# Attention exponentials shared between ScalarE and VectorE: a shorter polynomial with a phase in the row maxima, and another spacing of VectorE's sets

## The chip, the cores and the metric

The kernel runs on one core of a Trainium2 chip. The metric is the device time of one execution in microseconds (us); each version is run several times and the median is taken. Beside it there is one execution recorded by the hardware profiler, whose span and instructions are quoted here. TensorE (PE) multiplies matrices into PSUM, ScalarE (ACT) evaluates functions such as exp, VectorE (DVE) does elementwise arithmetic and reductions, GpSimd (POOL) copies and issues some DMAs, SyncE (SP) issues most DMAs.

## The reference

Four graph layers over 3327 nodes with 128 features and a 3327 x 3327 matrix adj. Nearly all the time is in the first, an attention of 128 heads with 8 features each, in which adj is added to the logits twice:

```python
def _L0_gnn_ref(x, spatial_encoding, edge_encoding, Wq, Wk, Wv, Wo):
    q = (x @ Wq.T).reshape(d, n, h)
    k = (x @ Wk.T).reshape(d, n, h)
    v = (x @ Wv.T).reshape(d, n, h)
    a = jnp.einsum('dnh,dmh->dnm', q, k) * scale
    a = a + spatial_encoding + edge_encoding
    a = jax.nn.softmax(a, axis=2)
    out = jnp.einsum('dnm,dmh->dnh', a, v)
    out = out.reshape(n, h * d)
    return out @ Wo.T
...
x = _layernorm(x + _L0_gnn_ref(x, adj, adj, Wq, Wk, Wv, Wo))
x = _layernorm(x + _L1_gnn_ref(x, adj, W, b))
x = _layernorm(x + _L2_gnn_ref(x, adj, W_in, W_out))
x = _layernorm(x + _L3_gnn_ref(x, adj, W, b))
```

So 128 x 3327 x 3327 exponentials are taken, about 1.4 thousand million.

## The kernel before

A first stage (to about 320 us) projects queries, keys and values and writes them to scratch memory in DRAM. It also stores, for 512 rows at a time, the row maxima of adj split in two parts (`store_tops`, L220 to L228); these go into the queries' image as extra rows, so that the matmul of the scores subtracts them. The last stage (from about 10000 us) runs the other layers. Between them `attention` (L412) holds the change.

**Tiling.** The queries are cut into seven columns of 476 (`CW`), the keys into four runs of 7, 7, 6 and 6 tiles of 128 (`KBS`). A *block* is one column with one run, 28 blocks in all; the kind of a block (`kb`, 0 to 3) is its run. Each block goes through all 128 heads, four heads making a *group* (`GROUP`), 32 groups a block.

**Sets.** For one head the key tiles of a block are taken in three *sets* (`SETS`, L446): 3, 2 and 2 tiles in blocks of seven, 2, 2 and 2 in blocks of six. Each set has its own PSUM buffer (`sc0`, `sc1`, `sc2`), only one of each. `exponents` (L609) issues, for one set, the score matmuls (L625) and then an exponential from PSUM to an SBUF tile `e`: on ScalarE (L633, with scale 2), or, for some third sets, on VectorE (`vector_exp`, L583). The scores stay in PSUM from head to head: each head's matmul adds its own product and takes the last head's away. So the matmul of the next head into a buffer must wait until the exponential has read it.

**VectorE's exponential.** L589 scales the scores to an integer (from PSUM), L590 and L592 separate exponent and mantissa, and one product for each constant of `POLY` follows (L595), five before. L589 is issued at once; the others are put in the list `vec`, and `vector_work` (L600) takes them out one by one, against a planner's clock: `clock[0]` advances a fixed amount a set (0.95 or 0.84 us), `clock[1]` by the estimated cost of VectorE's work. Tiles `ey` and `et` have one buffer each.

**Who takes a set.** `on_vector(kb, g)` (L448) gives VectorE the third set of a group's first head, in all groups of the second kind, in three of four of the first kind and in seven of eight of the last two.

**Weighing.** One group later `weigh` (L640) multiplies the exponentials of four heads with the values into the one PSUM buffer `o` (L651). Where in the group's twelve sets the weighings stand is given by tables: `FULL` for the first kind, `PLACES` for the others, `FIRST` for a block's first group (L455 to L458). Before a weighing that needs the third set, `weigh` takes the rest of that group's products out of `vec`. Every three groups `flush` (L658) adds `o` to an accumulator on VectorE (L662, L664), and the next weighing waits for that.

**Other work on VectorE in this stage.** In the groups ahead of a block of the first kind `copy_queries` (L506) makes three copies of the next group's queries (L510 to L512). `background_work` (L544) sums and transposes pieces of adj for the later layers: at the last head of every eighth group two operations (L202, L207), and four groups later three more (L209, L216, L217), for 91 pieces.

PE, ACT, POOL and DVE run in the order of this Python loop (`manual_schedule`): an instruction stands behind all that were issued before it on its engine.

Of the kernel before, what the change touches and what calls it, by code (L numbers as in the profile page):

```python
# [10 lines left out]
F32 = mybir.dt.float32  # L11
F32R = mybir.dt.float32r
I32 = mybir.dt.int32
AF = mybir.ActivationFunctionType
ALU = mybir.AluOpType
# [5 lines left out]
GROUP = 4  # L21
# [4 lines left out]
CW = 476  # L26
# [1 line left out]

POLY = (-0.12145248055458069, 1.287218689918518, 0.8447736501693726, 0.7106341123580933, 0.24892811477184296)
UPPER, LOWER = 0x7F800000, 0x7FFFFF
EXPONENT, QUARTER = 0x40000000, 0x3E800000
EPS = 1e-5
# [16 lines left out]
def kernel(ctx: ExitStack, tc: tile.TileContext, x, adj, wq, wk, wv, wo,  # L51
# [14 lines left out]
    nc = tc.nc  # L66
# [13 lines left out]
    KBS = [(0, 7), (7, 7), (14, 6), (20, 6)]  # L80
    assert KBS[-1][0] + KBS[-1][1] == T

    def tokens(t):
        return P - 1 if t == T - 1 else P
# [9 lines left out]
    def flat_ap(dram, at, pattern):  # L94

        f = dram.rearrange("r c -> (r c)")
        if isinstance(at, int):
            base = f[at:at + 1]
        else:
            base = f[ds(at, 1)]  # L100
        return bass.AP(base.tensor, base.offset, pattern)
# [118 lines left out]
    def store_tops(pool, u, top, n):  # L220

        hi = pool.tile([P, 4], F32R, name="rhi")
        nc.vector.tensor_copy(hi, top)
        lo = pool.tile([P, 4], F32R, name="rlo")
        nc.vector.tensor_tensor(lo, top, hi.bitcast(F32), ALU.subtract)
        for row, sb in enumerate((hi, lo)):
            for i in range(P // n):
                nc.gpsimd.dma_start(out=flat_ap(lead_s[u], row * SUPER + i * P, [[1, n], [n, 4]]),  # L228
                                    in_=sb[n * i:n * i + n, :].bitcast(F32))
# [18 lines left out]
    with tc.tile_pool(name="pw", bufs=1) as pw, tc.tile_pool(name="pa", bufs=2) as pa, \  # L248
# [110 lines left out]
        d = 0  # L359
# [30 lines left out]
        top = pw.tile([P, 2], F32, name="top")  # L390
# [21 lines left out]
    def attention():  # L412
        with tc.tile_pool(name="acc", bufs=1) as accp, tc.tile_pool(name="kq", bufs=3) as kq, \
# [14 lines left out]
            blocks = [(min(c, N - CW), kb) for c in range(0, N, CW) for kb in range(len(KBS))]  # L428
# [16 lines left out]

            SETS = {7: [(0, 3), (3, 2), (5, 2)], 6: [(0, 2), (2, 2), (4, 2)]}  # L446

            def on_vector(kb, g):  # L448

                return g % 4 != 0 if kb == 0 else KBS[kb][1] == 7 or g % 8 != 0  # L450

            FULL = ((0, 2, 4, 4, 7, 7, 9), (0, 0, 3, 7, 7, 10, 10), (0, 0, 3, 6, 6, 9, 9), (0, 0, 3, 6, 7, 10, 10))  # L455
            PLACES = {7: (1, 1, 4, 6, 8, 10, 10), 6: (0, 2, 4, 6, 8, 10)}

            FIRST = {7: (4, 4, 5, 7, 7, 10, 10), 6: (4, 4, 7, 7, 10, 10)}  # L458

# [54 lines left out]
            def tile_at(nt, i):  # L514

                return (i % 2, i // 2, (i // 2) + ((nt + 1) // 2 if i % 2 else 0))

            def load_values(b, g):
                k0, nt = KBS[blocks[b][1]]
                if g % 2 == 0:  # L520
                    pairs[b, g // 2] = kq.tile([P, 2, 7 * 32], F32, name="vs", bufs=2)
                    nc.sync.dma_start(out=pairs[b, g // 2].rearrange("p a c -> p (a c)")[:, 0:2 * nt * 32],
                                      in_=flat_ap(v_img, k0 * HD + g * nt * 32, [[T * HD, P], [1, 2 * nt * 32]]))
                vs = pairs[b, g // 2].rearrange("p a c -> p (a c)")[:, g % 2 * nt * 32:(g % 2 + 1) * nt * 32]
                vp = v_pads[(b * NHG + g) % 3]
                nc.gpsimd.tensor_copy(  # L526
                    vp[:, 32:32 + nt * GROUP * 32].rearrange("p (x c) -> p x c", c=32)[:, :, 0:H],
                    vs.rearrange("p (x c) -> p x c", c=H))
                return vp
# [27 lines left out]
            def prepare(b, d):  # L557

                n = b * NHG + d // GROUP
                if d % GROUP == 0:  # L560
                    while any(of is None for _, of, _ in vec):
                        vec.pop(0)[2]()
                    if n + 2 < len(groups):
                        heads[groups[n + 2]] = load_heads(*groups[n + 2])
                    if blocks[b][1] == 0:
                        nc.sync.dma_start(out=qimg[d // GROUP],
                                          in_=heads[groups[n]][1].bitcast(F32)[0:64].rearrange("p a c -> p (a c)"))
                    if n + 1 < len(groups):
                        values[groups[n + 1]] = load_values(*groups[n + 1])
                    while stores:  # L570
                        store(*stores.pop(0))
                    background(n)


                if n + 1 < len(groups) and blocks[groups[n + 1][0]][1] == 0 \
                        and d % GROUP == 1 - on_vector(blocks[b][1], d // GROUP):
                    vec.extend(copy_queries(*groups[n + 1]))
                if d % GROUP == 3:
                    background_work(n)

            vec = []

            def vector_exp(e, x, of):  # L583


                y = ex.tile([P, 2, CW], F32, name="ey")
                t = ex.tile([P, 2, CW], F32, name="et")
                yi, ti = y.bitcast(I32), t.bitcast(I32)
                nc.vector.tensor_scalar(yi, x, -58 * math.log(2.0), 2 ** 24 / math.log(2.0), ALU.max, ALU.mult)  # L589
                vec.append((0.7, of, lambda: nc.vector.tensor_scalar(ti, yi, UPPER, EXPONENT, ALU.bitwise_and,  # L590
                                                                 ALU.bitwise_xor)))
                vec.append((0.7, of, lambda: nc.vector.tensor_scalar(yi, yi, LOWER, QUARTER, ALU.bitwise_and,  # L592
                                                                 ALU.bitwise_or)))
                for i, a in enumerate(POLY):
                    vec.append((1.2, of, lambda i=i, a=a: nc.vector.scalar_tensor_tensor(  # L595
                        e, e if i else y, a, t if i == len(POLY) - 1 else y, ALU.add, ALU.mult)))

            clock = [0.0, 0.0]

            def vector_work(b):  # L600

                while vec and clock[1] < clock[0]:
                    cost, _, step = vec.pop(0)
                    step()
                    clock[1] += cost
                clock[0] += 0.95 if KBS[blocks[b][1]][1] == 7 else 0.84
                clock[1] = max(clock[1], clock[0] - 1)

            def exponents(b, d, si):  # L609
                kb = blocks[b][1]  # L610
                nt = KBS[kb][1]
                t0, n = SETS[nt][si]
                s = sc[si]
                if d == 0:
                    for i in range(n):
                        tl = tile_at(nt, t0 + i)[2]
                        for j, (q0, w) in enumerate(subs):
                            nc.tensor.matmul(s[:, i, q0:q0 + w], lhsT=edges[b][0:w, j, tl * P:(tl + 1) * P],
                                             rhs=ident[0:w, 0:w], is_transpose=True,
                                             start=(j == 0), stop=True, skip_group_check=True)  # L620
                kt, qt = heads[b, d // GROUP]
                k = d % GROUP
                for i in range(n):
                    rg, pos, _ = tile_at(nt, t0 + i)
                    nc.tensor.matmul(s[:, i, 0:CW], lhsT=kt[64 * rg:64 * rg + 64, k, pos * P:(pos + 1) * P],  # L625
                                     rhs=qt[64 * rg:64 * rg + 64, k, :],
                                     start=False, stop=True, skip_group_check=True)
                e = ex.tile([P, (3, 2, 2)[si], CW], F32, tag=f"e{si}", name=f"e{si}", bufs=(6, 7, 8)[si])
                if on_vector(kb, d // GROUP) and (d % GROUP, si) == (0, 2):
                    vector_exp(e[:, 0:n, :], s[:, 0:n, 0:CW], (b, d // GROUP))  # L630
                    clock[1] += 1.2
                else:
                    nc.scalar.activation(e[:, 0:n, :], s[:, 0:n, 0:CW], AF.Exp, scale=2.0)  # L633
                for i in range(n):
                    es[b, d, t0 + i] = e[:, i, :]
                if d % (2 * GROUP) == 0 and d // (2 * GROUP) < len(subs) and si == len(SETS[nt]) - 1 \
                        and b + 1 < len(blocks):
                    load_edges(b + 1, d // (2 * GROUP))
# [39 lines left out]
            with tc.manual_schedule(engines={mybir.EngineType.PE, mybir.EngineType.Activation,  # L678
# [8 lines left out]
                for b, d in steps:  # L687
                    prepare(b, d)
                    for si in range(len(SETS[KBS[blocks[b][1]][1]])):
                        vector_work(b)  # L690
                        exponents(b, d, si)
                        if queue:
                            at = (FIRST[len(queue_of)] if d < GROUP else PLACES[len(queue_of)] if blocks[b][1] else
                                  FULL[d // GROUP % 4])
# [462 lines left out]
    with tc.manual_schedule(engines={mybir.EngineType.PE, mybir.EngineType.SP}):  # L1157
# [18 lines left out]
        for t in range(T):  # L1176
            n = tokens(t)
# [15 lines left out]
        for t in range(T):  # L1193
            n = tokens(t)
# [15 lines left out]
        for t in range(T):  # L1210
            n = tokens(t)
# [16 lines left out]
        for t in range(T):  # L1228
            n = tokens(t)
# [35 lines left out]
```

## Time and profile before

| | |
|---|---|
| median of 3 runs | 10760.09 us (10756.05 to 10763.08) |
| span of the profiled execution | 10769.0 us |
| attention stage, first score tile to last weighing | 322 to 10001 us |
| ScalarE's exponentials (L633) | 9968 |
| VectorE's sets (L589) | 784 |
| mean granted TensorE clock | 0.994 |

A busy time is the time in which an engine has an instruction running. The profile gives after each group's busy time the engine's idle time just before it and what ended most of it. The windows view shows one block of each kind (the columns are the window, its length, busy time and instructions of each engine, the granted clock, the DMA share and GB/s):

```profile
1718.00:2085.00 367.00, 359.91 (x2705) 128.50 (x2703) 299.40 (x319) 362.95 (x361) 58.64 (x104) 1.00 0.67 174
2085.00:2453.00 368.00, 367.17 (x2720) 130.72 (x2716) 287.09 (x288) 356.24 (x353) 50.41 (x96) 1.00 0.86 193
2453.00:2775.00 322.00, 319.36 (x2342) 105.44 (x2338) 254.59 (x260) 308.70 (x357) 58.09 (x106) 1.00 0.90 203
2775.00:3095.00 320.00, 318.83 (x2334) 105.54 (x2333) 256.41 (x258) 309.24 (x358) 76.62 (x132) 1.00 0.89 208
```

The engines stand in the order PE, PE weight loads, DVE, ACT, POOL. Blocks of seven tiles take about 368 us, blocks of six about 320 us.

### The profile page before, as it was taken

Reading aid. Unit: us, or ns where it says so; the run is one execution under the profiler, and the core shown is the slowest. Engines: PE = TensorE matmul, PEld = TensorE weight load, DVE = VectorE, ACT = ScalarE, POOL = GpSimd, SP = SyncE. Lnnn points to the kernel's source line nnn. Section 1 sums busy time; section 2 is a strip of 40 time slices with the busy share of each in tenths; the row PEclk is TensorE's granted clock in tenths of the full one; section 3 lists DMA queues with packets and bytes.
Section 4 is the critical chain, followed back from the end, with each engine's and each line's share of the span. In section 5 each row is a group of like instructions: output and inputs, shape, how many; then the busy total and the mean of one; then the engine's idle time right before and its main releaser. Section 6 shows DMA issues by size and latency. Waiting matters only on the chain. (4 is left out here: it accounts for less than half of the span.)

```text
span 10769.0 us, 200811 instructions
## 1 busy us (share of the span) xinstructions
PE 10578.8 (98%) x76941; PEld 4110.9 (38%) x76941; DVE 7959.0 (74%) x8554; ACT 9583.6 (89%) x10447; POOL 1555.0 (14%) x2742
## 2 busy tenths in 40 slices
PE   8899999999999999999999999999999999999999
PEld 5333333333333333333333333333333333333779
DVE  6677788877788778887788777878777777777412
ACT  3799999999999999999999999999999999999400
POOL 0111122111221111211122111121111100001200
PEclk9999999999999999999999999999999999999999
DMA  7678897788976889768888688886888867888676
GB/s 250 187 183 189 205 212 183 178 194 199 211 191 168 199 203 209 192 170 193 198 209 200 156 192 189 198 195 171 194 194 201 195 162 178 181 188 197 220 281 246
DMA packets 1013555, 2116.45 MB, mean 197 GB/s; under 512 B 206760, under 2 KB 730730, under 8 KB 998772
## 3 DMA queue, kind: packets, MB, share of 16 engines
q1 hardware_dynamic: 915358, 1972.12, 75.8%
q0 software_dynamic: 79616, 116.88, 3.7%
q8 instruction: 623, 10.21, 0.4%
q10 hardware_dynamic: 17620, 14.49, 0.4%
q14 instruction: 338, 2.76, 0.1%
HBM read 1863.03 MB, written 239.54 MB: 195 GB/s over the span
## 5 line engine op out<-in xcount | busy, mean ns | idle before, releaser
L633 ACT ACTIVATE e<-sc 128x952 f32<-128x952 f32 (+1 forms) x9968 | 9361.2, 1085 | 322.8 <-PE sc L625 295.0
L651 PE MATMUL o<-e,v_pad 128*32 128x476 f32 (+1 forms) x46592 | 5650.9, 573 | 43.2 <-DVE acc L664 18.6
L625 PE MATMUL sc<-qt,kt 64*128 64x476 f32 x23296 | 4494.8, 440 | 55.8 <-ACT e L633 33.9
L625 PEld LDWEIGHTS sc<-qt,kt 64*128 64x128 f32 x23296 | 2184.3, 184 | 4439.7 <-ACT e L633 3736.3
L595 DVE SCALAR_TENSOR_TENSOR e<-e,ey 128x952 f32<-128x952 f32 x2352 | 2706.5, 1151 | 77.4
L589 DVE TENSOR_SCALAR ey<-sc 128x952 int32<-128x952 f32 x784 | 901.2, 1149 | 1426.5 <-PE sc L625 1389.1
L651 PEld LDWEIGHTS o<-e,v_pad 128*32 128x32 f32 (+1 forms) x46592 | 1035.8, 108 | 1914.8 <-issue 1893.1
L526 POOL COPY v_pad<-vs 128x192 f32<-128x192 f32 (+1 forms) x896 | 439.0, 516 | 8029.8 <-DMA vs<-v_img 6501.4
L595 DVE SCALAR_TENSOR_TENSOR e<-ey 128x952 f32<-128x952 f32 x784 | 903.0, 1152 | 27.2
L595 DVE SCALAR_TENSOR_TENSOR e<-e,et 128x952 f32<-128x952 f32 x784 | 901.5, 1150 | 22.2
L237 POOL DMA_DIRECT2D adjT_s<-at x1352 | 760.4, 570 | 141.5 <-DMA adjT_s<-at 99.2
L590 DVE TENSOR_SCALAR et<-ey 128x952 int32<-128x952 int32 x784 | 519.5, 663 | 26.9
L592 DVE TENSOR_SCALAR ey<-ey 128x952 int32<-128x952 int32 x784 | 518.9, 662 | 27.1
L1101 PE MATMUL bank<-y,eT 128*128 128x128 f32 (+1 forms) x4056 | 473.9, 276 | 0.4 <-DVE h L1223 0.4
L1101 PEld LDWEIGHTS bank<-y,eT 128*128 128x128 f32 (+1 forms) x4056 | 465.3, 192 | 5.7 <-DVE h L1223 0.6
L664 DVE TENSOR_TENSOR acc<-o,acc 128x476 f32<-128x476 f32 x231 | 150.3, 651 | 284.5 <-PE o L651 284.0
L510 DVE TENSOR_SCALAR qt<-qt 32x1428 fp32r<-32x1428 f32 x224 | 201.8, 901 | 93.3 <-DMA qt<-q_s 64.2
L1061 ACT ACTIVATE rstd<-mv,eps 128x1 f32<-128x1 f32 x104 | 30.4, 293 | 265.2 <-DVE mv L1059 265.2
L512 DVE CAST qt<-qt 64x1904 fp32r<-64x1904 f32 x224 | 259.9, 1160 | 7.6
L671 POOL DMA_DIRECT2D o_s<-acc x308 | 200.4, 655 | 35.3 <-DVE acc L664 21.2
L1204 PE MATMUL bank<-a,y 128*128 128x512 f32 (+2 forms) x364 | 145.5, 562 | 0.0
L348 ACT ACTIVATE hi<-pp 128x1024 fp32r<-128x1024 f32 x52 | 52.7, 1024 | 95.4 <-PE pp L292 78.2
(151 smaller groups left out, 2286.6 us busy)
## 6 DMA issues: line engine op xcount, KB each, us to landing
qt<-qimg SPq DMA_DIRECT2D x1344, 476.0 KB
kt<-k_s SPq DMA_DIRECT2D x5320, 96.0 KB
kt<-k_s SPq DMA_DIRECT2D x1764, 128.0 KB
eT<-adjT_s SPq DMA_DIRECT2D x78, 1664.0 KB
qimg<-qt SPq DMA_DIRECT2D x224, 476.0 KB
vs<-v_img SPq DMA_DIRECT2D x224, 224.0 KB
adjT_s<-at POOLq DMA_DIRECT2D x1352, 32.0 KB, 5.0
vs<-v_img SPq DMA_DIRECT2D x224, 192.0 KB
```

The lines of the kernel that those rows point to most:

```text
L237: nc.gpsimd.dma_start(out=flat_ap(adjT_s, (t * P + 32 * q) * NP + c * PIECE, [[NP, 32], [P, ns], [1, P]]), in_=at[32 * i:32 * i + 32].rear ...
L510: return [(0.9, None, lambda: nc.vector.tensor_scalar(qt[32:64, 1:], qf[0:32, 0:GROUP - 1], -1.0, None, ALU.mult)), (0.4, None, lambda: nc ...
L512: (1.2, None, lambda: nc.vector.tensor_copy(qt[64:128], qf[0:64]))]
L526: nc.gpsimd.tensor_copy(vp[:, 32:32 + nt * GROUP * 32].rearrange("p (x c) -> p x c", c=32)[:, :, 0:H], vs.rearrange("p (x c) -> p x c", c=H))
L589: nc.vector.tensor_scalar(yi, x, -58 * math.log(2.0), 2 ** 24 / math.log(2.0), ALU.max, ALU.mult)
L590: vec.append((0.7, of, lambda: nc.vector.tensor_scalar(ti, yi, UPPER, EXPONENT, ALU.bitwise_and, ALU.bitwise_xor)))
L592: vec.append((0.7, of, lambda: nc.vector.tensor_scalar(yi, yi, LOWER, QUARTER, ALU.bitwise_and, ALU.bitwise_or)))
L595: vec.append((1.2, of, lambda i=i, a=a: nc.vector.scalar_tensor_tensor(e, e if i else y, a, t if i == len(POLY) - 1 else y, ALU.add, ALU.m ...
L625: nc.tensor.matmul(s[:, i, 0:CW], lhsT=kt[64 * rg:64 * rg + 64, k, pos * P:(pos + 1) * P], rhs=qt[64 * rg:64 * rg + 64, k, :], start=False ...
L633: nc.scalar.activation(e[:, 0:n, :], s[:, 0:n, 0:CW], AF.Exp, scale=2.0)
L651: nc.tensor.matmul(o[32 * j:32 * j + 32, 0:CW], lhsT=values[b, g][:m, c:c + 32], rhs=es[b, g * GROUP + j, r][:m, :], start=(r == 0 and u = ...
L1101: nc.tensor.matmul(ps[:n, 0:D], lhsT=e[:m, s, :n], rhs=y[:m, s, col:col + D], start=(s == 0), stop=(s == T - 1))
```

## The change

VectorE's polynomial has four constants and products instead of five. A constant `PHASE` is taken off the stored row maxima, so that every score is higher by it; ScalarE's exponential takes twice that off again with its bias. `on_vector` now counts heads: VectorE takes the third set of every fourth head in the first kind of block, of every third head in the second, and of heads 0 and 4 of every seven in the last two. `vector_exp` first takes the products of an earlier set out of `vec`. The places of the weighings in blocks of six move by one set, the query copies enter at a group's first head in all groups, and the planner's clock advances by 0.935 and 0.81.

```diff
-POLY = (-0.12145248055458069, 1.287218689918518, 0.8447736501693726, 0.7106341123580933, 0.24892811477184296)
+POLY = (-0.039287679561190725, 0.7694055213858888, 0.3602062482980112, 0.1471829588776368)
+PHASE = 0.7927868171488225 * math.log(2.0) / 2
...
-        nc.vector.tensor_copy(hi, top)
+        nc.vector.tensor_scalar(hi, top, -PHASE, None, ALU.add)
...
-        nc.vector.tensor_tensor(lo, top, hi.bitcast(F32), ALU.subtract)
+        nc.vector.scalar_tensor_tensor(lo, top, -PHASE, hi.bitcast(F32), ALU.add, ALU.subtract)
...
-            def on_vector(kb, g):
-
-                return g % 4 != 0 if kb == 0 else KBS[kb][1] == 7 or g % 8 != 0
+            def on_vector(kb, d):
+
+                return d % 4 == 0 if kb == 0 else d % 3 == 0 if KBS[kb][1] == 7 else d % 7 in (0, 4)
...
-            PLACES = {7: (1, 1, 4, 6, 8, 10, 10), 6: (0, 2, 4, 6, 8, 10)}
+            PLACES = {7: (1, 1, 4, 6, 8, 10, 10), 6: (1, 3, 5, 7, 9, 11)}
...
                 if n + 1 < len(groups) and blocks[groups[n + 1][0]][1] == 0 \
-                        and d % GROUP == 1 - on_vector(blocks[b][1], d // GROUP):
+                        and d % GROUP == 0:
                     vec.extend(copy_queries(*groups[n + 1]))
...
             def vector_exp(e, x, of):
+                while any(to is not None for _, to, _ in vec):
+                    vec.pop(0)[2]()
...
-                clock[0] += 0.95 if KBS[blocks[b][1]][1] == 7 else 0.84
+                clock[0] += 0.935 if KBS[blocks[b][1]][1] == 7 else 0.81
...
-                if on_vector(kb, d // GROUP) and (d % GROUP, si) == (0, 2):
+                if si == 2 and on_vector(kb, d):
                     vector_exp(e[:, 0:n, :], s[:, 0:n, 0:CW], (b, d // GROUP))
                     clock[1] += 1.2
                 else:
-                    nc.scalar.activation(e[:, 0:n, :], s[:, 0:n, 0:CW], AF.Exp, scale=2.0)
+                    nc.scalar.activation(e[:, 0:n, :], s[:, 0:n, 0:CW], AF.Exp, bias=-2 * PHASE, scale=2.0)
```

## The prediction

> **What bounds the kernel now.** I read the busy shares first, then the groups by shape, then VectorE's and ScalarE's timelines inside the attention stage (320 to 10000 us, where the change lies), and last the waits of PE.
>
> ```profile
> PE 10578.8 (98%) x76941; PEld 4110.9 (38%) x76941; DVE 7959.0 (74%) x8554; ACT 9583.6 (89%) x10447; POOL 1555.0 (14%) x2742
> ```
>
> ```profile
> L633 ACT ACTIVATE e<-sc 128x952 f32<-128x952 f32 x8176 | 7324.3, 1015 | 202.3 <-PE sc L625 197.8
> L633 ACT ACTIVATE e<-sc 128x1428 f32<-128x1428 f32 x1792 | 2512.6, 1402 | 120.5 <-PE sc L625 97.2 <-DMA qt<-q_s 23.2
> L589 DVE TENSOR_SCALAR ey<-sc 128x952 int32<-128x952 f32 x784 | 901.2, 1149 | 1426.5 <-PE sc L625 1389.1
> L590 DVE TENSOR_SCALAR et<-ey 128x952 int32<-128x952 int32 x784 | 519.5, 663 | 26.9
> L592 DVE TENSOR_SCALAR ey<-ey 128x952 int32<-128x952 int32 x784 | 518.9, 662 | 27.1
> L595 DVE SCALAR_TENSOR_TENSOR e<-e,ey 128x952 f32<-128x952 f32 x2352 | 2706.5, 1151 | 77.4
> ```
>
> The first fence is the page's busy time, the second the groups by shape (busy us, mean ns of one, idle time before and its releaser). PE's 98% has modelled ends, so it does not say that PE is the limit. ScalarE is idle only 323 us before its exponentials. VectorE waits 1389 us for fresh scores before L589, 1.8 us for each of 784 sets: that is its slack. In time, in a block of six key tiles:
>
> ```profile
> 2577.34 1.15 DVE L589 TENSOR_SCALAR ey<-sc 128x952 int32<-128x952 f32 x1 [1.38 <-PE sc L625]
> 2583.35 1.24 DVE L202 STREAM_TRANSPOSE at<-ai 128x1024 f32<-128x1024 f32 x1
> 2584.51 1.18 DVE L207 TENSOR_REDUCE pmax<-ai 128x4 f32<-128x1020 f32 x1
> 2585.61 0.64 DVE L664 TENSOR_TENSOR acc<-o,acc 128x476 f32<-128x476 f32 x1
> 2588.13 1.15 DVE L589 TENSOR_SCALAR ey<-sc 128x952 int32<-128x952 f32 x1 [0.83 <-PE sc L625]
> ...
> 2597.97 1.15 DVE L589 TENSOR_SCALAR ey<-sc 128x952 int32<-128x952 f32 x1 [0.31 <-PE sc L625]
> ...
> 2605.27 1.15 DVE L595 SCALAR_TENSOR_TENSOR e<-e,et 128x952 f32<-128x952 f32 x1
> 2607.81 1.15 DVE L589 TENSOR_SCALAR ey<-sc 128x952 int32<-128x952 f32 x1 [1.39 <-PE sc L625]
> ...
> 2627.92 1.15 DVE L589 TENSOR_SCALAR ey<-sc 128x952 int32<-128x952 f32 x1 [8.68 <-PE sc L625]
> ```
>
> One L589 a group of four heads makes the starts a clock. 2597.97 to 2607.81 is 9.84 us: a group with one VectorE set. 2607.81 to 2627.92 is 20.11 us over two groups, the second without a set: 10.27 us. 2577.34 to 2588.13 is 10.79 us: here background work (L202, L207) stood ahead of the eviction L664. Its cost is visible on PE, and ScalarE's view of the set is this:
>
> ```profile
> 2586.39 1.01 PE L651 MATMUL o<-e,v_pad 128*32 128x476 f32 x8 [0.89 <-DVE acc L664]
> ```
>
> ```profile
> 2603.55 5.29 ACT L633 ACTIVATE e<-sc 128x952 f32<-128x952 f32 x6
> 2609.14 3.53 ACT L633 ACTIVATE e<-sc 128x952 f32<-128x952 f32 x4 [0.31 <-PE sc L625]
> ```
>
> ScalarE runs back to back (3.53 us for four, less 0.98 for the last one's own length, over three steps: 0.85; I use 0.843, the median distance of starts). When VectorE takes a set, ScalarE is relieved of 0.84 us and then idles 0.31 us, plus a pipeline fill, since PE has not run further ahead. The three score buffers let PE lead by about 0.3 us only. So PE and ScalarE pace each other, and neither is alone the limit.
>
> **What the Trainium skill says.** "Perfetto Trace Analysis", section "Identifying the Most-Contended Engine", says matmul busy time does not measure how near PE is to its roofline; the trace agrees: 98% here, while ScalarE paces it. "VectorE: DVE Perf Modes", section "Why PSUM operands drop a tier", has a PSUM operand hold fp32 at one element a cycle; the trace agrees: L589 from PSUM 1149 ns, L590 on as many SBUF elements 663. "ScalarE: Activation LUTs", section "What ACT_TABLE_LOAD costs", says that an immediate bias costs nothing and a pointer bias about 93 ns more. The program of the changed kernel has no new constant tile, so its bias is an immediate: nothing. If it were a pointer, 9,709 activations would cost up to 900 us; no trace of before shows it, and I exclude it on the operand's form.
>
> **The change, part by part.**
>
> Counts. A block has 128 heads; there are 7 blocks of each of the four kinds. Sets on VectorE a block: first kind 24 to 32, second 32 to 43, third and fourth 28 to 37 each. In all 784 to 1043, +259. The matmuls and the DMAs are the same, in number and in order on SP and POOL. On PE the six-tile weighings move one set later (places 0, 2, 4, ... become 1, 3, 5, ...): still six a group, with two sets between, so PE's own time stays, and the eviction after the last one keeps its distance to the weighing that waits for it. The row maxima (L223, L225) keep their number and shape: nothing.
>
> VectorE's work. A set now takes 1149+663+662+5x1151 = 8229 ns; one product less makes it 7078. 784x8.229 = 6452 us become 1043x7.078 = 7382: +930, so 7959 becomes 8890. With the gaps of the timeline (2597.97 to 2606.42, less the 1.18 of one product) a set holds the engine 7.27 us.
>
> What the relief is worth. ScalarE loses 259x0.843 = 218 us. But a set bought only 10.27-9.84 = 0.43 us of a six-tile group, since PE's lead is short. In six-tile blocks PE alone needs 9.40 us a group: its repeating pattern, two score sets and one weighing, takes 1.57 us when nothing stalls (score matmuls from 2606.99 to 2608.56), and a group has six of them. ScalarE lags 0.843-0.783 = 0.06 us a set, PE may lead 0.3, and each relief resets the lead. The excess over 9.40 in twelve sets is 0.72-12x0.29/n with a relief every n sets: 0.43 at n=12 (measured 9.84), 0.39 at n=10.5 (now). So 0.04x32x14 = 18 us gained. The first kind gets a set in its eight bare groups, worth about 0.25 us each (its L589 starts at 1825.53, 1837.24, 1848.41, 1871.44, 1882.83 lie 11.4 us apart on the mean, and 23.03 over two groups with a bare one, which leaves 11.6 for that): 8x0.25x7 = 14 us. In the second, one relief every nine sets could give 27 us by the same sum, but the weighings of L456 suit a set of the group's first head, and now it falls on every head in turn, once right before a weighing; I take 0 (from -30 to +27). Together -32; at most -60 by these sums, -90 at the old worth a set.
>
> What VectorE's lateness costs. Heads between sets become 3 or 4. In six-tile blocks three heads last 3x2.46 = 7.4 us, against 7.27 of work: slack 0.1; four heads leave 2.6. Second kind: 3x2.84 = 8.5, slack 1.25. First: 11.4-7.27-2.5 (query copies, L510 to L512) = 1.6. Into this fall bursts that the change keeps: 91 pieces, each with L202+L207 (2.26 us) and later L209+L216+L217 (2.54 us), 182 bursts, half of them in six-tile blocks, and 308 evictions of 0.57. Before, a burst was hidden by slack of about 1.4 to 2.5, except where an eviction followed: +0.95 (10.79 against 9.84). Now in six-tile blocks the cover is gone: the next L589 starts 1 to 2 us late, and PE, which wants that score buffer again three sets later, tolerates 0.2 to 1.1; or the eviction is late and the next weighing waits; what remains meets the following set. I take 0.95 for each: 91x0.95 = 86 us (from 35, if half the bursts find the four-head gap, to 150). Evictions within a three-head gap: 11 a block x 3/7 x 14 = 66, 0.2 each: 13. A set of a group's last head now must be ready ten sets later (L456's new places gave one set more): 10x0.82-0.5 = 7.7 us against 7.3 to 7.9 with an eviction; nine such sets a block, a third late by 0.3: 13. Second kind: 45 bursts at 0.3: 14; first kind 0. L583's new loop puts all products of the old set ahead of the next L589; before, a late last product could follow it (2589.19 after 2588.13), so a late L589 is later by up to 1.15 us more, which is why I don't take less than 0.95 for a burst. The planner's rates (0.935, 0.81) and the query copies that now always enter at a group's first head only shift products among VectorE's waits: 0, within 15 us either way. Sum +126.
>
> Net +126-32 = +94, say +90. Against the profiled execution 10769 becomes 10859; that lies 9 us above the median of the runs (10760), so the median becomes 10850.
>
> **Rivals.**
> 1. The relief is worth as much as before. For it: 0.43 us measured a set. Against: a second relief within twelve sets finds less lag. 126x0.43+133x0.25 = 87 us less, bursts hidden: 10673. This is the other side; it decides if VectorE's lateness stays within PE's tolerance.
> 2. PE comes free: six-tile groups reach 9.40 from a mean of 9.89: 0.49x32x14 = 220, 10540. Against: VectorE would need 37x7.27+26 = 295 us of 301.
> 3. Gain and lateness cancel: 10765.
> 4. Lateness feeds itself, since each late L589 starts the next chain late: twice the 126 without gain, 11010.
>
> **How the numbers follow.** Forecast 0.62, rival 1 0.13, rival 2 0.05, rival 3 0.08, rival 4 0.12. The forecast's own range, from the bounds of the burst cost and the relief, is 10785 to 10920. The range 10690 to 10935 leaves out rivals 2 and most of 1 and 4, two in ten. A change under 0.2% (22 us) can't be told from none. Faster 0.18, same 0.08, slower 0.74.
>
> **What would show it.** VectorE near 8890 us and 1043 of its first step; ScalarE's activations 9709, its idle time before L633 above 450 us instead of 323, so that the relief turns into waiting; six-tile blocks near 325 us instead of 320; PE waits for L589's successor and for the eviction longer than 1 us. Wrong if six-tile groups fall to 9.6 us or less, or if activations get longer.

## The result and the profile after

| | before | changed |
|---|---|---|
| median | 10758.07 us (4 runs, 10751.05 to 10763.08) | 10814.59 us (4 runs, 10805.89 to 10819.29) |
| span of the profiled execution | 10769.0 us | 10817.4 us |
| VectorE's sets | 784 | 1043 |
| ScalarE's exponentials | 9968 | 9709 |

The ratio is 1.0049, with a 95% interval from 1.0037 to 1.0061: the changed kernel is slower, by about 56 us. Its line numbers lie three higher from here on: L589 became L592, L595 became L598, L625 L628, L633 L636, L651 L654, L664 L667; L202 and L207 became L203 and L208.

The page's busy time, and then the groups by shape (busy us and mean ns of one; after the second bar, idle time before and what ended it):

```profile
PE 10482.2 (97%) x76941; PEld 4007.7 (37%) x76941; DVE 8862.6 (82%) x9583; ACT 9440.2 (87%) x10188; POOL 1710.5 (16%) x2742
```

```profile
L636 ACT ACTIVATE e<-sc 128x952 f32<-128x952 f32 x7917 | 7120.3, 991 | 381.9 <-PE sc L628 362.8
L654 PE MATMUL o<-e,v_pad 128*32 128x476 f32 x44800 | 5439.3, 573 | 80.6 <-DVE acc L667 70.1 <-POOL v_pad L527 6.9 <-DVE e L598 0.7
L628 PE MATMUL sc<-qt,kt 64*128 64x476 f32 x23296 | 4378.3, 437 | 163.2 <-ACT e L636 79.9 <-DVE ey L592 67.9 <-DVE qt L512 4.8
L636 ACT ACTIVATE e<-sc 128x1428 f32<-128x1428 f32 x1792 | 2474.6, 1381 | 131.5 <-PE sc L628 128.3
...
L592 DVE TENSOR_SCALAR ey<-sc 128x952 int32<-128x952 f32 x1043 | 1196.9, 1148 | 870.5 <-PE sc L628 847.5 <-ACT e L636 18.5
```

VectorE is busy 904 us longer (8862.6 less 7959.0). ScalarE's exponentials take less time, but its idle time before them has grown from 323 to 513 us (381.9 + 131.5): most of the 218 us that it was relieved of came back as waiting for PE. PE now waits on VectorE in two places where it hardly did: 67.9 us for L592 to read the score buffer (1.8 us before), and 70.1 us for the eviction, which takes `o` to the accumulator (29.3 us before, L662 and L664 together). The kernel before in the view of waits (total us, number, longest):

```profile
PE sc L625 <- DVE ey L589: 1.8, 5, 0.6
PE o L651 <- DVE acc L664: 18.6, 38, 1.7
PE o L651 <- DVE acc L662: 10.7, 35, 0.9
```

Of the 67.9 us, 8.0 are a single wait at 6041.6, where VectorE itself had just stood idle 11.18 us for a transfer of queries; that is no lateness of the sets. Without it the two growths make 99 us. VectorE waited 1389 us for scores in 687 of 784 sets; now it waits 847.5 us in 611 of 1043. In 28 of the others its wait ended with an exponential of ScalarE, and 404 start with no wait above 0.15 us (82 before).

The same in time, VectorE's timeline in a six-tile block of the changed kernel (start, duration, instruction, and in brackets the idle time before and its releaser):

```profile
2582.98 1.15 DVE L592 TENSOR_SCALAR ey<-sc 128x952 int32<-128x952 f32 x1 [2.38 <-PE sc L628]
...
2590.22 1.14 DVE L592 TENSOR_SCALAR ey<-sc 128x952 int32<-128x952 f32 x1
...
2592.68 1.25 DVE L203 STREAM_TRANSPOSE at<-ai 128x1024 f32<-128x1024 f32 x1
...
2595.39 0.65 DVE L667 TENSOR_TENSOR acc<-o,acc 128x476 f32<-128x476 f32 x1 [0.36 <-PE o L654]
...
2600.57 1.14 DVE L592 TENSOR_SCALAR ey<-sc 128x952 int32<-128x952 f32 x1
...
2607.79 1.14 DVE L592 TENSOR_SCALAR ey<-sc 128x952 int32<-128x952 f32 x1
```

The sets at 2590.22, 2600.57 and 2607.79 have no bracket: VectorE came from other work, and the scores may have been ready for some time. From 2582.98 to 2590.22 are three heads, 7.24 us, which is about what a set takes.

Not every burst of background work costs much. The one at 2592.68 falls between two sets that are four heads apart: of the two groups behind it the first takes as long as in a block without background work (9.80 and 9.81 us), the second 0.4 us longer. A burst between sets three heads apart, in the same block (VectorE's and PE's timelines):

```profile
2546.60 1.15 DVE L592 TENSOR_SCALAR ey<-sc 128x952 int32<-128x952 f32 x1 [2.31 <-PE sc L628]
2552.60 1.21 DVE L210 TENSOR_REDUCE psum<-ai 128x4 f32<-128x1024 f32 x1
2553.73 1.21 DVE L217 TENSOR_REDUCE cs<-at 128x8 f32<-128x1024 f32 x1
2556.12 1.14 DVE L592 TENSOR_SCALAR ey<-sc 128x952 int32<-128x952 f32 x1
```

```profile
2557.32 0.70 PE L628 MATMUL sc<-qt,kt 64*128 64x476 f32 x4 [1.50 <-DVE ey L592]
2558.89 0.70 PE L628 MATMUL sc<-qt,kt 64*128 64x476 f32 x4
```

The set at 2556.12 has to stand behind L210 and L217, PE waits 1.50 us for it, and this group takes 11.95 us where it takes 9.82 without background work. Of PE's waits for L592, 41 are longer than 1 us (none before): 33 stand behind the three bursts with only three heads between the sets in each of eleven six-tile blocks, 6 at the borders of blocks (see the run with none in the last heads), and 2 elsewhere.

**Where the time went, by block.** The edge transposes (L618, now L621) open a block, so their first starts give its length. Two blocks of the third kind, one with background work on VectorE and the last, where all 91 pieces are done. PE's timeline before:

```profile
3831.21 1.04 PE L618 MATMUL sc<-ident,e_in 128*128 128x128 f32 x8
...
4151.53 1.04 PE L618 MATMUL sc<-ident,e_in 128*128 128x128 f32 x8
...
9358.49 1.04 PE L618 MATMUL sc<-ident,e_in 128*128 128x128 f32 x8
...
9677.80 1.04 PE L618 MATMUL sc<-ident,e_in 128*128 128x128 f32 x8
```

and after:

```profile
3848.09 1.04 PE L621 MATMUL sc<-ident,e_in 128*128 128x128 f32 x8
...
4171.73 1.04 PE L621 MATMUL sc<-ident,e_in 128*128 128x128 f32 x8
...
9407.91 1.04 PE L621 MATMUL sc<-ident,e_in 128*128 128x128 f32 x8
...
9725.36 1.04 PE L621 MATMUL sc<-ident,e_in 128*128 128x128 f32 x8
```

With background work 320.32 us became 323.64, without it 319.31 became 317.45. So the change gains 1.9 us in such a block where VectorE has nothing else to do, and background work costs 6.2 us a block now instead of 1.0. Over the seven blocks of each kind, from the first to the fourth kind, the mean length changed by +0.6, +1.8, +3.1 and +1.5 us, 49 us in all, which is the difference of the spans.

### The profile page after: what moved, and what is told of

It is laid out like the page before. It is cut to its first block, busy times and chain, and to the rows that moved or that the text cites. A ratio compares the mean times of both kernels' runs of the same rounds, so it can differ in the third digit from the quotient of the medians.

```text
span 10817.4 us, 202137 instructions
## 1 busy us (share of the span) xinstructions
PE 10482.2 (97%) x76941; PEld 4007.7 (37%) x76941; DVE 8862.6 (82%) x9583; ACT 9440.2 (87%) x10188; POOL 1710.5 (16%) x2742
## 5 line engine op out<-in xcount | busy, mean ns | idle before, releaser
L636 ACT ACTIVATE e<-sc 128x952 f32<-128x952 f32 (+1 forms) x9709 | 9217.4, 1063 | 513.4 <-PE sc L628 491.1
L654 PE MATMUL o<-e,v_pad 128*32 128x476 f32 (+1 forms) x46592 | 5663.0, 573 | 80.6 <-DVE acc L667 70.1
L628 PE MATMUL sc<-qt,kt 64*128 64x476 f32 x23296 | 4378.3, 437 | 163.2 <-ACT e L636 79.9
L628 PEld LDWEIGHTS sc<-qt,kt 64*128 64x128 f32 x23296 | 2076.0, 184 | 4459.9 <-ACT e L636 3708.3
L598 DVE SCALAR_TENSOR_TENSOR e<-e,ey 128x952 f32<-128x952 f32 x2086 | 2407.4, 1154 | 69.3
L592 DVE TENSOR_SCALAR ey<-sc 128x952 int32<-128x952 f32 x1043 | 1196.9, 1148 | 870.5 <-PE sc L628 847.5
L527 POOL COPY v_pad<-vs 128x192 f32<-128x192 f32 (+1 forms) x896 | 601.6, 695 | 7930.5 <-DMA vs<-v_img 5680.7
L654 PEld LDWEIGHTS o<-e,v_pad 128*32 128x32 f32 (+1 forms) x46592 | 1039.5, 108 | 2040.4 <-issue 1987.5
L598 DVE SCALAR_TENSOR_TENSOR e<-ey 128x952 f32<-128x952 f32 x1043 | 1202.8, 1153 | 40.5 <-DVE ey L595 0.9
L598 DVE SCALAR_TENSOR_TENSOR e<-e,et 128x952 f32<-128x952 f32 x1043 | 1201.9, 1152 | 31.9
L595 DVE TENSOR_SCALAR ey<-ey 128x952 int32<-128x952 int32 x1043 | 688.7, 660 | 36.0
L593 DVE TENSOR_SCALAR et<-ey 128x952 int32<-128x952 int32 x1043 | 688.7, 660 | 32.8
L667 DVE TENSOR_TENSOR acc<-o,acc 128x476 f32<-128x476 f32 x231 | 150.0, 649 | 72.8 <-PE o L654 72.6
```

The costliest lines, as they stand in the source:

```text
L527: nc.gpsimd.tensor_copy(vp[:, 32:32 + nt * GROUP * 32].rearrange("p (x c) -> p x c", c=32)[:, :, 0:H], vs.rearrange("p (x c) -> p x c", c=H))
L654: nc.tensor.matmul(o[32 * j:32 * j + 32, 0:CW], lhsT=values[b, g][:m, c:c + 32], rhs=es[b, g * GROUP + j, r][:m, :], start=(r == 0 and u = ...
```

## The experiments

Theory A is that of the forecast: a further set off ScalarE is worth little, and VectorE, left with almost no slack where its sets lie three heads apart, is late when background work or an eviction falls in. The rivals are named with each run. Ratios are to the kernel before, measured beside each run. Its median there lay between 10758 and 10769 us, and at 10758 beside the changed kernel, so the difference of two rows, or of a row and the changed kernel, is uncertain by about 10 us. Groups are numbered from 0 within a block, and the length of a group runs from its first score matmul to the next group's, as a median over the blocks of a kind.

| run | median us | ratio, 95% interval |
|---|---|---|
| polynomial alone | 10751.64 | 0.9987 [0.9980, 0.9993] |
| every fourth head | 10695.63 | 0.9935 [0.9921, 0.9948] |
| old places | 10898.02 | 1.0122 [1.0107, 1.0138] |
| background work spread | 10765.61 | 1.0000 [0.9991, 1.0008] |
| two products | 10722.96 | 0.9961 [0.9948, 0.9975] |
| no set on VectorE | 11137.31 | 1.0345 [1.0329, 1.0360] |
| every fourth in the second kind | 10787.10 | 1.0020 [1.0013, 1.0027] |
| every fourth, spread, old places | 10705.88 | 0.9945 [0.9931, 0.9958] |
| every fourth, work moved | 10697.72 | 0.9941 [0.9927, 0.9955] |
| none in the last heads | 10806.16 | 1.0043 [1.0029, 1.0057] |
| two products, old places | 10766.00 | 0.9997 [0.9989, 1.0005] |

**The polynomial alone.** The kernel before with the new constants, the phase and the bias, nothing else.

```diff
-POLY = (-0.12145248055458069, 1.287218689918518, 0.8447736501693726, 0.7106341123580933, 0.24892811477184296)
+POLY = (-0.039287679561190725, 0.7694055213858888, 0.3602062482980112, 0.1471829588776368)
...
-                    nc.scalar.activation(e[:, 0:n, :], s[:, 0:n, 0:CW], AF.Exp, scale=2.0)
+                    nc.scalar.activation(e[:, 0:n, :], s[:, 0:n, 0:CW], AF.Exp, bias=-2 * PHASE, scale=2.0)
```

> The kernel before with the four-constant polynomial and the phase alone; the 784 sets, their heads, the places and the clock stay. Theory A (VectorE's lateness is the cost, ScalarE's relief is worth little): only 784 x 1.15 = 902 us of VectorE work go, and with them the few late evictions of before; 10730 to 10755, so 0 to 28 us below 10758. Theory B (the phase or the biased exponential itself slows ScalarE): above 10775. Theory C (VectorE's amount of work was already a limit before): below 10700.

Measured 10751.64 us: 15 us less, as A has it. VectorE's busy time fell from 7959 to 7078 us, and 881 us of spared work bought 15, as it would if nearly all of that work lay in slack; PE's waits for the eviction fell by as much (29.3 to 14.8 us). Theory C falls too. ScalarE's busy time stayed (9583.6 and 9580.3 us): phase and bias cost ScalarE nothing, and theory B falls.

**Every fourth head.** The changed kernel with the sets regular again.

```diff
-                return d % 4 == 0 if kb == 0 else d % 3 == 0 if KBS[kb][1] == 7 else d % 7 in (0, 4)
+                return d % 4 == 0
```

> The changed kernel with VectorE's set at every fourth head in all blocks (896 sets instead of 1043). Theory A: the four-head gap hides every burst again and the bare groups are gone; 10720 to 10755, at or below the kernel before. Theory B (more relief of ScalarE is what helps, and the loss comes from something else, such as the places or the order of products): 147 sets less make it slower than the changed kernel, above 10815.

Measured 10695.63 us, 119 us below the changed kernel with 147 sets fewer, and below the lower end of what A had expected. Theory B falls. It is the fastest kernel of the study and beats both. VectorE's timeline there, with the same background work:

```profile
2560.14 1.15 DVE L592 TENSOR_SCALAR ey<-sc 128x952 int32<-128x952 f32 x1 [2.48 <-PE sc L628]
...
2566.15 1.24 DVE L203 STREAM_TRANSPOSE at<-ai 128x1024 f32<-128x1024 f32 x1
...
2568.40 0.64 DVE L667 TENSOR_TENSOR acc<-o,acc 128x476 f32<-128x476 f32 x1
...
2570.72 1.15 DVE L592 TENSOR_SCALAR ey<-sc 128x952 int32<-128x952 f32 x1 [0.62 <-PE sc L628]
```

Even with L203, L208 and an eviction between them, the next set finds VectorE idle for 0.62 us: in a four-head gap the set isn't late. The burst isn't wholly hidden, though, for it stands ahead of the eviction, and PE waits for that:

```profile
2569.19 1.00 PE L654 MATMUL o<-e,v_pad 128*32 128x476 f32 x8 [0.76 <-DVE acc L667]
```

This group, number 13, takes 10.42 us, and number 25, also behind an eviction, 10.64; most of the others take 9.74. PE's matmuls waited 15.3 us for L592 and 26.1 us for the eviction in that run (67.9 and 70.1 in the changed kernel; 8.1 of the 15.3 is the like stop behind a transfer).

**Old places.**

```diff
-            PLACES = {7: (1, 1, 4, 6, 8, 10, 10), 6: (1, 3, 5, 7, 9, 11)}
+            PLACES = {7: (1, 1, 4, 6, 8, 10, 10), 6: (0, 2, 4, 6, 8, 10)}
```

> The changed kernel with the old places (0, 2, 4, 6, 8, 10) of the weighings in six-tile blocks. Theory A with the readiness term of the forecast (a set of a group's last head is needed one set sooner, nine sets a block, 14 blocks): slower than the changed kernel by 40 to 90 us, 10855 to 10905, and PE waits for the last product appear. Theory B (the new places cost, since they shift the eviction): faster than the changed kernel, below 10800.

Measured 10898.02 us, 83 us above the changed kernel, as A has it. In the last block of the third kind, where no background work disturbs, its edge transposes start at 9468.48 and the next block's at 9793.07: 324.59 us against 317.45. The weighings' weight loads wait for the last products (L598), here and then in the changed kernel:

```profile
PEld o L654 <- DVE e L598: 100.5, 141, 1.3
```

```profile
PEld o L654 <- DVE e L598: 9.5, 16, 1.5
```

These waits grow by 91 us. So one set of time more for the last products is worth 7 us in such a block, once sets fall on a group's last heads, and the change needs it.

**Background work spread.** The five operations of a piece in four groups, two groups apart.

```diff
                     worked.append((u, c, next(steps)))
-                    next(steps)
-                    clock[1] += 2.4
-                    turning.append(steps)
-                if n % PACE == 0 and turning:
-                    clock[1] += 2.4
-                    for _ in turning.pop():
-                        pass
+                    clock[1] += 1.2
+                    turning.append([steps, 3])
+                elif n % 2 == 0 and turning:
+                    next(turning[0][0])
+                    clock[1] += 1.2
+                    turning[0][1] -= 1
+                    if not turning[0][1]:
+                        for _ in turning.pop(0)[0]:
+                            pass
```

> The changed kernel with the background work cut in four parts, one or two operations in each of four groups two groups apart, instead of two bursts of 2.3 and 2.5 us. The work is the same. Theory A (bursts without cover): most of the loss in the six-tile blocks goes; 10760 to 10785, about 30 to 55 us below the changed kernel. Theory B (VectorE's amount of work or the spacing of the sets as such, not bursts): within 10 us of 10815.

Measured 10765.61 us, 49 us below the changed kernel with the same work on VectorE (8846.7 us). The block that took 323.64 us takes 319.70 (3828.38 to 4148.08 by its edge transposes). So most of the 56 us of loss comes from the bursts standing together, and not from the amount of work.

**Two products.** Two of VectorE's four products are left out, so its values are no exponentials and the time of a set falls by 2.3 us; all else is the changed kernel.

```diff
-POLY = (-0.039287679561190725, 0.7694055213858888, 0.3602062482980112, 0.1471829588776368)
+POLY = (-0.039287679561190725, 0.1471829588776368)
```

> The changed kernel with two of the four products of VectorE's exponential left out (its values are no exponentials then; the sets, their heads and all else stay). VectorE has 1043 x 2.3 = 2400 us less to do, so lateness is gone and what is left is the worth of the relief. Theory A (the forecast's own sum: relief 32 us, at most 60): 10695 to 10735. Rival (a set is worth as much as before, 87 us): 10665 to 10680. Theory C (the relief at three- and four-head spacing is worth nothing, since the sets fall at places where PE blocks or ScalarE starves anyway): 10745 or more. If VectorE's lateness is not the cause of the loss: about 10815.

Measured 10722.96 us: 92 us below the changed kernel and about 40 below the kernel before. It splits the change in two terms: with VectorE's work made short, about 40 us gained; through its length, about 92 us lost. The groups by shape show which wait went:

```profile
L654 PE MATMUL o<-e,v_pad 128*32 128x476 f32 x44800 | 5419.5, 573 | 69.5 <-DVE acc L667 63.3 <-POOL v_pad L527 4.1
L628 PE MATMUL sc<-qt,kt 64*128 64x476 f32 x23296 | 4377.4, 437 | 103.8 <-ACT e L636 81.0 <-DVE ey L592 8.9 <-DVE qt L512 4.9
```

The wait for L592 fell from 67.9 to 8.9 us (all of it the one stop behind a transfer), while that for the eviction stayed (63.3). The bursts that still stand ahead of it are only part of the reason, for with the bursts spread it is 48.1 us; the rest is open. So the run doesn't remove all lateness, and 92 us is a lower bound of it.

**No set on VectorE.**

```diff
-                return d % 4 == 0 if kb == 0 else d % 3 == 0 if KBS[kb][1] == 7 else d % 7 in (0, 4)
+                return False
```

> The changed kernel with no set on VectorE at all: ScalarE takes all 10752. It shows what the first 784 sets are worth to the kernel before. Theory A (0.43 us a set in six-tile blocks, 0.25 in seven-tile blocks, as the bare groups show): 392 x 0.43 + 392 x 0.25 = 267 us above 10766, 11000 to 11060. Theory B (ScalarE is the limit and a set is worth its whole 0.84 us): 784 x 0.84 = 660 above, 11400.

Measured 11137.31 us: the first 784 sets are worth 374 us, 0.48 each. Theory B (0.84 each) falls, but A had expected 0.34. The gap lies in the seven-tile blocks. The time from a group's first score matmul to the next group's (median over seven blocks) is 11.87 us in the second kind without a set and 11.36 with one, 0.51; and in the first kind 12.31 against 11.50 in every second group, 0.81. In six-tile blocks it is 10.28 against 9.83, as in the bare groups.

**Every fourth in the second kind alone.**

```diff
-                return d % 4 == 0 if kb == 0 else d % 3 == 0 if KBS[kb][1] == 7 else d % 7 in (0, 4)
+                return d % 4 == 0 if KBS[kb][1] == 7 else d % 7 in (0, 4)
```

> The changed kernel with every fourth head instead of every third in the second kind of block alone (966 sets). Theory A (the denser sets bring the second kind nothing and cost a little): its blocks go from 371.5 us to about 368, in all 10785 to 10800. Theory B (they help there): slower than the changed kernel, above 10820.

Measured 10787.10 us, 27 us less, with 77 sets fewer. The blocks of that kind fell from 371.5 to 368.3 us, as A has it, 22 of the 27 us. Lateness is the smaller part of this: with two products, where no set's length presses, they still take 370.5 us, 2.2 more than here. At every third head the sets are a loss there even when VectorE's work is short.

**Every fourth, spread, old places.** The `d % 4 == 0` of the run with every fourth head, with the spread work and the old places.

> The changed kernel with a set at every fourth head in all blocks, the background work in four parts, and the old places of the weighings in six-tile blocks. Theory A (what is left of lateness at every fourth head is the bursts in front of an eviction, groups 13 and 25 of six-tile blocks, 10.4 and 10.6 us instead of 9.74): 10660 to 10690, below the run with every fourth head (10696). Theory B (the bursts are hidden there already and the new places are what made it fast): 10700 or more.

Measured 10705.88 us, 10 us above the run with every fourth head: the time is B's, the mechanism only in part. Groups 13 and 25 came down to 9.83 us, so the bursts had not all been hidden, as A said, but every other six-tile group takes 9.83 us instead of 9.74. The kernel before, with the old places and the work not spread, has 9.83 too, so with sets at every fourth head it is the new places that are worth 0.09 us a group.

**Every fourth, work moved.** The run with every fourth head, and in the groups whose end has an eviction the work is issued at the first head.

```diff
-                if d % GROUP == 3:
+                if d % GROUP == (0 if d // GROUP % 3 == 0 else 3):
                     background_work(n)
```

> The run with a set at every fourth head, with the background work in groups whose number divides by three (where an eviction follows at the group's end) issued at the group's first head instead of its last. Theory A (what is left there is a burst in front of an eviction, groups 13 and 25 of six-tile blocks at 10.4 and 10.6 us): these two come down to 9.74 and the time falls by 1.6 us in each of about eleven blocks, 18 us, to 10670 to 10685. Theory B (the work costs wherever it stands): within 8 us of 10696.

Measured 10697.72 us, no gain over 10695.63. Groups 13 and 25 did come down to 9.75 us, but in the fourth kind group 12 rose to 16.25. VectorE's timeline there:

```profile
2877.42 1.25 DVE L203 STREAM_TRANSPOSE at<-ai 128x1024 f32<-128x1024 f32 x1 [4.51 <-DMA adjT_s<-at]
...
2879.68 1.14 DVE L592 TENSOR_SCALAR ey<-sc 128x952 int32<-128x952 f32 x1
```

Moved three heads ahead, L203 came before the last piece had been stored from `at`, the buffer that it writes; VectorE stood idle for 4.51 us, and L592 behind it was late. The new place was right in one respect and wrong in another, and the run doesn't decide between A and B as they were put.

**None in the last heads.**

```diff
-                return d % 4 == 0 if kb == 0 else d % 3 == 0 if KBS[kb][1] == 7 else d % 7 in (0, 4)
+                return d < 124 and (d % 4 == 0 if kb == 0 else d % 3 == 0 if KBS[kb][1] == 7 else d % 7 in (0, 4))
```

> The changed kernel without VectorE's sets at heads 124 and above of a block (1015 sets), so that no set stands two heads ahead of the next block's first one. Theory A (the two-head gap together with the query copies makes a block of the first kind start late, its first two groups 13.3 and 12.8 us instead of 12.1 and 11.4): those fall back, 2.6 us in each of six blocks, less what the sets were worth; 10795 to 10805. Theory B (the slow start comes from the copies entering earlier, not from the gap): within 8 us of 10815.

Measured 10806.16 us, 8 us less: at the border of what either theory expected by time. The trace decides it. In the changed kernel VectorE's timeline at the start of a block of the first kind is

```profile
1718.56 1.15 DVE L592 TENSOR_SCALAR ey<-sc 128x952 int32<-128x952 f32 x1 [0.38 <-PE sc L628]
...
1721.10 1.15 DVE L513 CAST qt<-qt 64x1904 fp32r<-64x1904 f32 x1
...
1728.54 1.13 DVE L592 TENSOR_SCALAR ey<-sc 128x952 int32<-128x952 f32 x1
...
1730.95 1.15 DVE L513 CAST qt<-qt 64x1904 fp32r<-64x1904 f32 x1
...
1741.02 1.15 DVE L592 TENSOR_SCALAR ey<-sc 128x952 int32<-128x952 f32 x1
```

Head 126's set at 1718.56 is two heads ahead of the next block's first one; with the query copies in between, of which the blocks of the first kind need three a group, VectorE takes 9.98 us from the one to the other, and the backlog reaches the set after. Without it, the block's first two groups take 11.89 and 11.76 us instead of 13.31 and 12.79. Its last group, now without a set, takes 13.77 instead of 12.97, which gives part back. So the two-head gap is the main cause of the slow start; the copies' early entry alone is not, since it stayed.

**Two products, old places.**

The two edits shown above, together.

> The changed kernel with two of the four products of VectorE's exponential left out (its values are no exponentials then) and with the old places of the weighings in six-tile blocks. VectorE is not late in either kernel, so the difference to the run with two products (10723) is the worth of the new places alone. Theory A (the places are worth 0.09 us a group, as six-tile groups show between the two runs with every fourth head, 9.74 and 9.83): 448 x 0.09 = 40 us slower, about 10763, and the denser sets as such are worth nothing. Theory B (the forecast's: the places cost and bring nothing, the denser sets bring the 40 us): within 8 us of 10723.

Measured 10766.00 us, the number of theory A, but not by its mechanism. Little of the 43 us is spread over all groups: in the third kind's last block, without background work, the places make 0.3 us (318.15 against 317.86). Most comes from group 13, which takes 12.77 us instead of 9.86, since PE waits there for an eviction behind a burst:

```profile
2583.37 1.00 PE L654 MATMUL o<-e,v_pad 128*32 128x476 f32 x8 [1.68 <-DVE acc L667]
```

That is most of the 3.3 us by which the third kind's mean block is longer. In that last block the denser sets with the old places gain 1.2 us on the kernel before (318.15 against 319.31), the new places 0.3 more. How the 40 us of the run with two products divide elsewhere, where bursts and evictions fall in, stays open.

## Why the prediction was right, and where it was not

Forecast 10850, measured 10814.59, within the range, slower as forecast. The mechanism held: relief worth little, and more than eaten up by VectorE's lateness. The forecast of +90 lies 34 us above the +56 measured. The price of the bursts was 29 us too high; the borders of blocks, 15 us, were left out, and this partly hid it.

- **VectorE's work.** +930 us was forecast, +904 measured in busy time, and the activations got no longer (a mean of 991 ns instead of 1015 for the two-tile form). That the bias costs nothing held, as the run with the polynomial alone shows.
- **Relief, -32 us.** About 40 with two products, the new places included. In six-tile blocks 18 was forecast, 1.3 us a block; the last block of the third kind shows 1.2 from the sets with the old places, and 1.9 in the changed kernel with the new ones, which makes 26 in 14 blocks. In the second kind I took 0, from a doubt that the weighing places suit only the first head's set; that doubt was right, and a little more: its last block takes 370.6 us against 368.5 without any background work. A set in a bare group of the first kind was put at 0.25 us (the starts quoted give 0.2) and brought 0.12 to 0.22 (11.50 us became 11.38, 11.67 became 11.46). As the worth of a set in all seven-tile blocks, as rival 1 and the run without sets took it, this was wrong: 0.5 to 0.8. The bare groups have other weighing places than their neighbours, and without any set they take 11.50 us where their neighbours take 11.93 to 12.31, so the comparison mixed two effects.
- **"PE's own time stays" with the new places.** Right for PE's pattern (1.57 us from 2557.32 to 2558.89; six of them are 9.42 us, not quite the 9.40 of the sum), wrong as a price of 0 for the whole: at every fourth head they bring 0.09 us a group, and with the new spacing they save about 83 us, which goes with the readiness of the last products. I had priced readiness at 13 us with the new places, and the changed kernel shows 9.5 us of weight loads waiting on L598.
- **Lateness, +126 us.** At least 92 (two products). The largest term, 0.95 us a burst in six-tile blocks, 86 us in all, was the one mis-sized: background work costs 6.2 us a block now and 1.0 before, so 5.2 us in each of the 11 six-tile blocks that have it, 57 us or 0.63 a burst; 49 us of the change's loss went with the bursts spread. I had taken one late eviction as the price of every burst, but only some cost anything. Three of a block's eight bursts fall into a three-head gap, between heads 18 and 21, 32 and 35, 81 and 84; the groups behind them (5, 9, 21) are 1.5, 2.1 and 1.2 us longer than in the third kind's last block. Of the five in four-head gaps, the two ahead of an eviction cost 0.4 and 0.7 us, the others at most 0.2.
- **Second kind, 14 us of bursts.** Its blocks are 1.0 us longer than with two products, 7 us in all. The 13 us for evictions in three-head gaps were not measured by themselves.
- **First kind, 0.** The spacing within a block was reckoned, the border between blocks not: two heads, with two rounds of query copies in them. It costs about 2.6 us (the first two groups, less the same groups before) in each of six blocks, 15 us, and hides the gain of the eight bare groups there.
- **Rival 1** (a set is worth as before, 87 us) fell: 40 us even with VectorE's work short. **Rival 2** (PE comes free) fell: six-tile groups stay near 9.8 us, not 9.40. **Rival 4** (lateness feeds itself) fell by the time; a backlog that reaches a further set was seen at the border of blocks. **Rival 3** (10765) fell too.

The signs I had named: VectorE near 8890 us (8863), ScalarE's idle time above 450 us (513), six-tile blocks near 325 us (323.6), PE's waits longer than 1 us, for the read of scores (41, none before) and for the eviction (19, 3 before). All came.

The planner's clock, and the loop at the head of `vector_exp` by itself, were not tried.

## What to carry to other kernels

When two engines hand buffers to each other, ask what a relieved engine does next: here ScalarE got back 0.84 us a set and waited for most of it. An engine that works in the gaps of others is priced by its shortest gap, not by its busy share: VectorE at 82% was late where it had been on time at 74%, and the same 82% with its background work in smaller parts cost 49 us less. Regular spacing of fewer sets (every fourth head, 896 of them, with the change's polynomial and places) beat both the kernel before and the denser change.

## What had not been expected of the hardware

GpSimd's copies of the values take longer beside some of VectorE's instructions and not beside others, at unchanged shape. The groups of that line, before, after, and with no set on VectorE:

```profile
L526 POOL COPY v_pad<-vs 128x192 f32<-128x192 f32 (+1 forms) x896 | 439.0, 516 | 8029.8 <-DMA vs<-v_img 6501.4 <-PE sc L625 1457.5 <-PE o L651 32.9
```

```profile
L527 POOL COPY v_pad<-vs 128x192 f32<-128x192 f32 (+1 forms) x896 | 601.6, 695 | 7930.5 <-DMA vs<-v_img 5680.7 <-PE sc L628 1809.8 <-PE o L654 419.5
```

```profile
L527 POOL COPY v_pad<-vs 128x192 f32<-128x192 f32 (+1 forms) x896 | 317.8, 377 | 8530.8 <-DMA vs<-v_img 6449.3 <-PE sc L628 1444.6 <-PE o L654 616.4
```

516 ns became 695, and 377 without sets. VectorE's busy share does not set this: with two products it is 60% and a copy takes 561 ns, with every fourth head 74% and 472 ns. What VectorE does just then decides. Two pairs of copies before, one beside the read of scores from PSUM, one beside products from SBUF:

```profile
2577.27 0.64 POOL L526 COPY v_pad<-vs 128x192 f32<-128x192 f32 x2 [9.47 <-PE sc L625]
2577.34 1.15 DVE L589 TENSOR_SCALAR ey<-sc 128x952 int32<-128x952 f32 x1 [1.38 <-PE sc L625]
```

```profile
2592.93 3.52 DVE L595 SCALAR_TENSOR_TENSOR e<-e,ey 128x952 f32<-128x952 f32 x3
2595.67 2.19 POOL L526 COPY v_pad<-vs 128x192 f32<-128x192 f32 x2 [17.76 <-DMA vs<-v_img]
2596.48 1.17 DVE L595 SCALAR_TENSOR_TENSOR e<-e,et 128x952 f32<-128x952 f32 x1
```

Over the whole run before, the 120 copies beside nothing of VectorE's but L589 and the 140 beside its reductions, transposes and evictions took as long as with VectorE idle, to within 12 ns (about 350 ns, or 376 for 128x224). The 260 slowed copies started while a product (L595), one of the integer steps L590 and L592 or a query copy was running, and they end about 0.2 us after that instruction, so that one takes up to 1.39 us. Why these instructions hold a copy back and the others don't, no run here shows. The copies are hardly on the path: PE's weighings waited 10.3 us for them before and 6.9 after.
